# Moving one message and one distance step between the last filter products of a graph layer, and building the factors in one piece

## The chip, the cores and the metric

The kernel runs on one core of a Trainium2 chip. The metric is the device time of one execution in microseconds (us). The engines named here are TensorE (PE in the profile; its weight loads are PEld), VectorE (DVE), ScalarE (ACT), GpSimd (POOL) and SyncE (SP, which here only issues transfers). Each engine works through its own instructions in program order, and they wait for each other through semaphores.

## The reference, cut to what matters

There are 64 graphs of 256 nodes with 256 channels each. The layer normalizes, then computes a convolution branch, a message branch that is weighted by distances, and a GRU gate over both.

```python
h = jnp.maximum(_layernorm(x, axis=-1), 0.0)          # the layer's input, called x below
# convolution branch: 1x1, then 17 taps along the nodes
c = relu(bn1(conv1d(xc, conv1_w, 0)))
x_conv = relu(bn2(conv1d(c, conv2_w, 8)) + xc)
# message branch: 3 distance coordinates s of each node
s = x @ w_se.T + b_se
sq = jnp.sum(s * s, axis=-1)
dist = sq[:, :, None] + sq[:, None, :] - 2.0 * jnp.einsum('bnd,bmd->bnm', s, s)
A = jnp.exp(-dist) * mask                              # mask is adj
msg = relu(x @ w_msg.T + b_msg)
x_nmp = jnp.einsum('bnm,bmd->bnd', A, msg)
# gates
gi = concatenate([x_conv, x_nmp]) @ w_ih.T + b_ih
gh = x @ w_hh.T + b_hh
# ... r, z, n as in a GRU; out = x_input + (1 - z) * n + z * x
```

## The kernel before: the parts that are touched

The kernel takes graphs in pairs (G = 2), four pairs to a block, eight blocks. The 17 taps are evaluated by a fast transform over 16 positions: VectorE transforms a whole block, TensorE multiplies it by transformed filters (`products`, eight steps per block), and VectorE transforms back. The transformed filters are made once at the start by TensorE, in 57 small steps (`filter_steps`), and parked in DRAM (`filt`); each block reads them back (`wb`, nine buffers).

One filter step, with five `acc` buffers in PSUM and six `fo` buffers:

```python
def filters(m, g, eng):
    p = acc()
    for dc in range(DC):
        mm(p[...], points[m][...], taps[:size * TAPS, g, dc, :], D, start=True, stop=True)
    t = stage.tile([P, W], FP, name="fo", bufs=6)
    nc.scalar.copy(t[:size * kinds], p[:size * kinds])
    eng.dma_start(out=filt[m][...], in_=t[:size * kinds])   # gpsimd and sync in turn
```

The message of a pair, its distance factors, their transposition and the distances. `Z` holds the factors with nodes on partitions, `ZT` with factors on partitions; a block of 32 columns of `Z` belongs to one of the four chunks of 128 nodes of the pair:

```python
Z = const.tile([P, 2, G * MC, Q], FP, name="z")             # MC = 2 chunks, Q = 32
ZT = const.tile([P, (1 + MC) * P], FP, name="zT")

def message(i):
    for g in range(G):
        for c in range(MC):
            p = acc() if g * MC + c == 3 else aux()
            for k in range(DC):
                mm(p[:, :D + SE], chunk(HT[i][:, k], g, c), w_msg[:, k, :], ...)
            pace.vector(D, pace.pe + PSUM)
            nc.vector.tensor_add(MSG[i][:, g, c, :], p[:, :D + SE], b_msg)
    s = MSG[i][:, :, :, D:]
    flat = s.rearrange("p g c s -> p (g c) s")
    nc.scalar.mul(Z[:, 0, :, :SE], flat, -2.0)
    nc.scalar.activation(Z[:, 0, :, SE:2 * SE], flat, AF.Square)
    nc.scalar.copy(Z[:, 1, :, :SE], flat)
    nc.scalar.activation(Z[:, 1, :, 2 * SE:KD], flat, AF.Square)
    for g in range(G):
        nc.scalar.activation(MSG[i][:, g, :, :D], MSG[i][:, g, :, :D], AF.Relu)

def embed(i):
    p = aux()
    for j in range(2):
        transpose(p[:, j * P:(j + 1) * P], Z[:, j].rearrange("p q s -> p (q s)"))
    nc.scalar.copy(ZT[:, :P], p[:, :P])
    for q in range(G * MC):
        for c in range(MC):
            m = q // MC * MC + c
            nc.scalar.copy(ZT[q * Q:(q + 1) * Q, (1 + c) * P:(2 + c) * P], p[m * Q:(m + 1) * Q, P:2 * P])

def affinity(i):
    for g in range(G):
        for c in range(MC):                                  # q = g * MC + c
            nc.tensor.matmul(p[:, :N], ZT[rows_q, :P], ZT[rows_q, P:], start=True, stop=True)
            nc.scalar.activation(E[i][:, g, c], p[:, :N], AF.Exp, scale=-1.0)
    # ... VectorE multiplies the four results by adj
    if i + 1 < BY_DMA:
        load_adj(i + 1)                                      # issued by gpsimd into the one adj buffer
```

VectorE's order is set while the program is built. `pace` keeps an estimated clock of TensorE and of VectorE, and `pace.vector` puts queued transform steps ahead of an operation as long as they fit before the operation's input is ready.

The end of the start-up, and the first part of a block:

```python
forward()                                       # queues the first block's transform for VectorE
filter_steps(len(steps) - (NG - FIRST) - 4)     # 17 of the 57 steps are left after this
for n in range(3):
    for kind in range(3):
        load_kind(0, n, kind)                   # nine wb reads of 256 KB, by sync
filter_steps(len(steps))
# ...
pace.flush(odd)
for b in range(NB):
    i = b * PB
    message(i)
    pace.flush(odd)
    products(b, 0)
    embed(i)
    products(b, 1)
    pace.add(fft.branch_back(Yv, T, 0))
    affinity(i)
    if b > 0:
        load_adj(i + 1)
    products(b, 2)
    # ... further products, three more pairs' messages, the gates of four pairs
```

The third pair of each block has its `embed` and `affinity` inside the first gate, just before the convolution result `Yv` of the block's first pair is joined, scaled (DVE L788) and passed through a relu (ACT L789) for the gate product.

Of the kernel before, what the change touches and what calls it, by code (L numbers as in the profile page):

```python
# [13 lines left out]
FP = mybir.dt.float32  # L14
U16 = mybir.dt.uint16
AF = mybir.ActivationFunctionType
# [285 lines left out]
def kernel(  # L302
# [26 lines left out]
    nc = tc.nc  # L329
    P = 128  # L330
    B, N, D = x.shape
    G = 2
# [4 lines left out]
    MC = N // P  # L337
    W = G * N
    TAPS = c2_wT.shape[1]
    SE = se_wT.shape[1]  # L340
    KD = 3 * SE
    Q = 32
# [6 lines left out]
    const = ctx.enter_context(tc.tile_pool(name="const", bufs=1))  # L349
# [255 lines left out]
    s1, h1_shift = fold_bn(bn1, "bn1")  # L605


    Z = const.tile([P, 2, G * MC, Q], FP, name="z")
    nc.gpsimd.memset(Z, 0.0)
    nc.gpsimd.memset(Z[:, 0, :, 2 * SE:KD], 1.0)  # L610
    nc.gpsimd.memset(Z[:, 1:, :, SE:2 * SE], 1.0)
    ZT = const.tile([P, (1 + MC) * P], FP, name="zT")
# [110 lines left out]
    def load_kind(b, n, kind):  # L723
        b, n = b + n // BINS, n % BINS
        if b < NB and (n < BINS - 1 or kind < 2):
            WB[b, n, kind] = work.tile([P, DC, D], FP, name="wb", bufs=9)
            m = n // len(PASSES[0])
            nc.sync.dma_start(out=WB[b, n, kind], in_=filt[m][:, 3 * (n - PASSES[m][0]) + kind])
# [63 lines left out]
    def message(i):  # L792
        MSG[i] = work.tile([P, G, MC, D + SE], FP, name="msg")
# [4 lines that stand above are left out]
                    mm(p[:, :D + SE], chunk(HT[i][:, k], g, c), w_msg[:, k, :], D + SE,  # L798
                       start=(k == 0), stop=(k == DC - 1))
# [3 lines that stand above are left out]
        flat = s.rearrange("p g c s -> p (g c) s")  # L803
        nc.scalar.mul(Z[:, 0, :, :SE], flat, -2.0)
        nc.scalar.activation(Z[:, 0, :, SE:2 * SE], flat, AF.Square)
        nc.scalar.copy(Z[:, 1, :, :SE], flat)
        nc.scalar.activation(Z[:, 1, :, 2 * SE:KD], flat, AF.Square)
        for g in range(G):
            nc.scalar.activation(MSG[i][:, g, :, :D], MSG[i][:, g, :, :D], AF.Relu)

    def embed(i):
        p = aux()
        for j in range(2):
            transpose(p[:, j * P:(j + 1) * P], Z[:, j].rearrange("p q s -> p (q s)"))
        nc.scalar.copy(ZT[:, :P], p[:, :P])
        for q in range(G * MC):
            for c in range(MC):
                m = q // MC * MC + c  # L820
                nc.scalar.copy(ZT[q * Q:(q + 1) * Q, (1 + c) * P:(2 + c) * P], p[m * Q:(m + 1) * Q, P:2 * P])  # L821


    def affinity(i):
        E[i] = work.tile([P, G, MC, N], FP, name="e")
        for g in range(G):
            for c in range(MC):
                q = g * MC + c
                p = acc() if q == 3 else aux()
                rows_q = slice(q * Q, q * Q + KD)  # L830
                nc.tensor.matmul(p[:, :N], ZT[rows_q, :P], ZT[rows_q, P:], start=True, stop=True)  # L831
                nc.scalar.activation(E[i][:, g, c], p[:, :N], AF.Exp, scale=-1.0)
        pace.tensor(N)
        for g in range(G):
            for c in range(MC):
                pace.vector(N, pace.pe + ACT)
                e = E[i][:, g, c].rearrange("p (c h b) -> p c h b", c=MC, b=NW)
                nc.vector.tensor_mul(e, e, ADJ[i][:, g * MC + c].rearrange("p (b h c) -> p c h b", c=MC, b=NW))
        AT[i] = E[i]
        if i + 1 < BY_DMA:  # L840
            load_adj(i + 1)
# [113 lines left out]
    def filter_steps(n):  # L955
        for k in range(n):
            filters(*steps.popleft(), nc.gpsimd if len(steps) % 2 else nc.sync)
# [29 lines left out]
    for n in range(3):  # L987
        for kind in range(3):
            load_kind(0, n, kind)
    filter_steps(len(steps))  # L990
    stage_ctx.close()
    late = ctx.enter_context(tc.tile_pool(name="late", bufs=1, reuse_waits="tile"))
# [3 lines left out]
    for b in range(NB):  # L996
        i = b * PB
        nxt = i + PB
        message(i)
        pace.flush(odd)  # L1000
        products(b, 0)
        embed(i)
        products(b, 1)
        pace.add(fft.branch_back(Yv, T, 0))
        affinity(i)
        if b > 0:
            load_adj(i + 1)
        products(b, 2)
        if b > 0:
            finish(i - 1)  # L1010
        else:
            transpose_a(i)
        products(b, 3)
        pace.flush(even)
        if b == 0:
            norm(nxt)
        else:
            run(norm_steps(nxt + 1)[0])
        pace.add(fft.branch_back(Yv, T, 2))
        pace.add(fft.odd_back(Yv, T))  # L1020
        aggregate(i)
        if b > 0:
            join_adj(i + 1)
        else:
            nc.gpsimd.dma_start(out=w_hh, in_=hh_wT.rearrange("(k p) o -> p k o", p=P))
            nc.gpsimd.dma_start(out=w_ih, in_=ih_wT.rearrange("(k p) o -> p k o", p=P))
        products(b, 4)
        message(i + 1)
        products(b, 5, lambda i=i: embed(i + 1))
        pace.add(mix(fft.q_back(Yu, T), fft.odd_factors(Yv)))  # L1030
        if b == 0:
            pace.add(norm_steps(nxt + 1)[0], normed[1])
        affinity(i + 1)
        if b > 0:
            load_adj(i + 2)
            join_h(nxt)
        products(b, 6)
        if b == 0:
            transpose_a(i + 1)
            transpose_h(nxt)  # L1040
        products(b, 7)
        pace.add(mix(fft.p_back(Yu, T), fft.q_factors(Yu)), scaled)

        def join(j):
            pace.add(fft.join(Yu, Yv, T, slice(2 * G * j, 2 * G * (j + 1))))
            pace.add([(W, lambda o=o: residual(i + j, o)) for o in range(DC)], joined[j])
        join(0)
        pace.add(norm_steps(nxt + 2)[0], normed[2])
        join(1)
        if b == 0:  # L1050
            turn_adj(3)
            keep_adj(3)
        aggregate(i + 1)
        if b > 0:
            join_adj(i + 2)
        message(i + 2)
        pace.flush(normed[1])
        turn_h(nxt + 1)

        def wait():  # L1060
            pace.flush(scaled)
            affinity(i + 2)
            conv1(nxt, aux)
            pace.add(split_steps(nxt), halved)
            join(2)
            pace.flush(joined[0])
        gates(i, 0, wait, lambda i=i: embed(i + 2))
        if b == 0:
            transpose_a(i + 2)
            load_y(0)  # L1070
        load_adj(i + 3)
        sort_h(nxt + 1)
        turn_adj(nxt)
        keep_adj(nxt)

        def early():
            join_h(nxt + 1)
            pace.flush(normed[2])
            turn_h(nxt + 2)
        gates(i, 1, None, early)  # L1080
        pace.flush(halved)
        conv1(nxt + 1)
        join(3)
        pace.add(split_steps(nxt + 1), halved)
        pace.add(norm_steps(nxt + 3)[0], normed[3])
        aggregate(i + 2)
        join_adj(i + 3)
        pace.flush(joined[1])
        sort_h(nxt + 2)
        turn_adj(nxt + 1)  # L1090
        keep_adj(nxt + 1)
        gates(i + 1, 0, lambda nxt=nxt: join_h(nxt + 2))
        pace.flush(normed[3])
        turn_h(nxt + 3)
        pace.flush(halved)
        conv1(nxt + 2)
        pace.add(split_steps(nxt + 2), halved)
        pace.add(norm_steps(nxt + 4)[0], normed[0])
        finish(i)
        sort_h(nxt + 3)  # L1100
        turn_adj(nxt + 2)
        keep_adj(nxt + 2)
        gates(i + 1, 1)
        join_h(nxt + 3)
        message(i + 3)
        conv1(nxt + 3)
        pace.add(split_steps(nxt + 3), halved)
        if b + 1 < NB:
            forward()
        pace.flush(normed[0])  # L1110
        pace.flush(joined[2])

        def wait():
            affinity(i + 3)
            turn_h(nxt + 4)
        gates(i + 2, 0, wait, lambda i=i: embed(i + 3))
        sort_h(nxt + 4)
        turn_adj(nxt + 3)
        keep_adj(nxt + 3)
        aggregate(i + 3)  # L1120
        finish(i + 1)
        load_adj(nxt)
        gates(i + 2, 1)
        join_adj(nxt)
        pace.flush(joined[3])
        gates(i + 3, 0)
        finish(i + 2)
        gates(i + 3, 1)
# [45 lines left out]
```

## Time and profile before

| | before |
|---|---|
| time, median of 3 runs | 1835.29 us (1831.43 to 1835.35) |
| span of the profiled execution | 1833.5 us |
| TensorE matmul busy | 1793.6 us (98%) |
| VectorE busy | 1366.9 us (75%) |
| ScalarE busy | 765.7 us (42%) |
| GpSimd busy | 219.2 us (12%) |
| first product of the first block starts at | 107.06 us |
| length of each of the blocks two to seven | 215.87 us |

The profile has a page of sums for the whole span (busy time per engine, the span in slices, the chain of work that ended last, the costliest groups of instructions) and views that can be asked for a stretch: a timeline of one engine's instructions, the waits (who waited for whom), and windows (busy time by stretch, with the clock granted to TensorE as a share of full speed and the share of time the DMA engines were busy). In a timeline line, the first number is the start, the second the length from the first start to the last end, then engine, source line, operation, destination and source, shapes and count; brackets hold idle time before it and what ended that. Source line L517 is the helper through which nearly all matmuls go, so tiles tell them apart. Each fp32 matmul of the program appears as more than one record.

### The profile page before, as it was taken

How to read it: one execution, taken by the hardware profiler on the slowest of the kernel's cores; microseconds unless marked ns; L12 is line 12 of the kernel's file. 1: busy time of each engine (PE TensorE's matmuls, PEld its weight loads, DVE VectorE, ACT ScalarE, POOL GpSimd, SP SyncE). 2: the span in 40 equal slices, each digit the busy share in tenths (PEclk: the TensorE clock that was granted, in tenths of full speed). 3: DMA queues.
4: the chain of work that ended last, by engine and by line, in shares of the span. 5: the costliest groups of instructions: out<-in, count | busy, mean ns of one | idle time of the engine just before them, and what ended most of it. 6: DMA issues, size and time to landing. Idle time of an engine off the chain costs nothing.

```text
span 1833.5 us, 21931 instructions
## 1 busy us (share of the span) xinstructions
PE 1793.6 (98%) x7462; PEld 1108.4 (60%) x7462; DVE 1366.9 (75%) x2596; ACT 765.7 (42%) x1508; POOL 219.2 (12%) x357
## 2 busy tenths in 40 slices
PE   5999999999999999999999999999999999999998
PEld 3687454964559454784448645595546944487453
DVE  4879669795879849797697967888587984979422
ACT  2535541364323643255422653246432464225321
POOL 2210101100111011111012000110111110111000
PEclk9999999999999999999999999999999999999999
DMA  7778543854438444574347544384554744164011
GB/s 196 235 245 233 125 97 88 240 149 111 106 93 265 105 103 93 148 198 121 81 97 216 165 95 110 84 264 120 114 96 122 225 105 96 41 186 114 7 40 34
DMA packets 250483, 245.96 MB, mean 134 GB/s; under 512 B 142936, under 2 KB 176500, under 8 KB 250371
## 3 DMA queue, kind: packets, MB, share of 16 engines
q1 hardware_dynamic: 216634, 183.83, 36.5%
q0 software_dynamic: 30784, 58.07, 13.8%
q10 hardware_dynamic: 2953, 2.66, 0.7%
q8 instruction: 59, 0.97, 0.2%
q14 instruction: 53, 0.43, 0.1%
HBM read 156.56 MB, written 44.30 MB: 110 GB/s over the span
## 4 chain that ended last, share of the span: by engine, by line
PE 85%; ACT 5%; DVE 4%; issue 3%; DMA 1%; POOL 1%; ACTq 0%; POOLq 0%; DVEq 0%
PE acc L517 73%; PE aux L517 9%; PE aux L521 2%; ACT Yv L68 1%; ACT zT L821 1%; ACT adj L426 1%; PE aux L831 1%; ACT hh L648 1%; ACT V L68 1%; DVE Yv L65 1%; DMA taps<-in_c_wT_dram 1%; POOL filt L717 0%; DVE V L65 0%; DMA filt<-fo 0%; DVE T L62 0%
## 5 line engine op out<-in xcount | busy, mean ns | idle before, releaser
L517 PE MATMUL acc<-xnm,w_ih 128*128 128x512 f32 x768 | 353.1, 592 | 0.0
L517 PE MATMUL acc<-hT,w_hh 128*128 128x512 f32 x768 | 350.5, 592 | 0.0
L517 PE MATMUL acc<-Yv,w_ih 128*128 128x512 f32 x768 | 343.4, 597 | 6.7 <-ACT Yv L789 6.7
L517 PEld LDWEIGHTS acc<-Yv,w_ih 128*128 128x128 f32 x768 | 145.2, 191 | 192.7 <-issue 177.3
L517 PEld LDWEIGHTS acc<-xnm,w_ih 128*128 128x128 f32 x768 | 144.7, 190 | 176.0 <-issue 174.6
L517 PEld LDWEIGHTS acc<-hT,w_hh 128*128 128x128 f32 x768 | 143.9, 190 | 164.6 <-issue 155.5
L891 ACT ACTIVATE tr<-acc,b_rz 128x512 f32<-128x512 f32 x64 | 44.0, 687 | 346.6 <-PE acc L517 345.7
L893 DVE SCALAR_TENSOR_TENSOR gn<-tr,gn 128x512 f32<-128x512 f32 x64 | 44.2, 691 | 192.5 <-ACT tr L891 192.3
L927 POOL DMA_DIRECT2D out_dram<-y x62 | 38.2, 620 | 787.4 <-DVE y L926 762.3
L517 PE MATMUL acc<-V,wb 128*128 128x128 f32 x1024 | 124.8, 275 | 0.0
L517 PE MATMUL acc<-U,wb 128*128 128x128 f32 x1024 | 124.2, 276 | 0.0
L517 PEld LDWEIGHTS acc<-U,wb 128*128 128x128 f32 x1024 | 120.0, 192 | 3.6 <-DVE T L59 2.0
L59 DVE SCALAR_TENSOR_TENSOR V<-T,V 128x256 f32<-128x256 f32 (+2 forms) x224 | 121.7, 612 | 0.3
L517 PEld LDWEIGHTS acc<-V,wb 128*128 128x128 f32 x1024 | 119.5, 192 | 0.0
L517 PE MATMUL acc<-hT,w_c 128*128 128x512 f32 x228 | 107.4, 612 | 1.9 <-ACT hT L633 1.9
L517 PE MATMUL aux<-e,msg 128*128 128x256 f32 x464 | 104.9, 379 | 0.0
L517 PEld LDWEIGHTS aux<-e,msg 128*128 128x128 f32 x464 | 87.1, 190 | 17.7 <-issue 6.9
L898 ACT ACTIVATE nn<-gn,bn_columns 128x512 f32<-128x512 f32 x64 | 46.2, 722 | 115.5 <-DVE gn L896 115.5
L565 POOL TENSOR_TENSOR rstd<-rstd,neg_half 128x4 f32<-128x4 f32 x32 | 37.6, 1176 | 472.2 <-DVE shift L567 343.8
L517 PE MATMUL aux<-w_msg,hT 128*128 128x259 f32 x384 | 89.5, 382 | 0.0
L517 PEld LDWEIGHTS aux<-w_msg,hT 128*128 128x128 f32 x384 | 72.1, 190 | 17.5 <-issue 7.6
L426 ACT COPY adj<-adjh 128x1024 uint16<-128x1024 uint16 x58 | 74.0, 1346 | 19.3 <-DMA adjh<-halves_d 19.3
(164 smaller groups left out, 2725.8 us busy)
## 6 DMA issues: line engine op xcount, KB each, us to landing
wb<-filt SPq DMA_DIRECT2D x376, 256.0 KB
y<-in_x_dram POOLq DMA_DIRECT2D x64, 256.0 KB, 5.4
out_dram<-y POOLq DMA_DIRECT2D x62, 256.0 KB, 5.7
x<-in_x_dram SPq DMA_DIRECT2D x60, 256.0 KB
halves_d<-halves SPq DMA_DIRECT2D x116, 128.0 KB
adjh<-halves_d POOLq DMA_DIRECT2D x116, 128.0 KB, 5.6
hh<-halves SPq DMA_DIRECT2D x108, 128.0 KB
filt<-fo POOLq DMA_DIRECT2D x18, 252.0 KB, 5.3
```

What stands on the lines that cost most here:

```text
L59: return self.step(out, lambda: self.v.scalar_tensor_tensor(out, x, s, y, op0=ALU.mult, op1=ALU.add))
L65: return self.step(out, lambda: self.v.tensor_sub(out, x, y))
L68: return 0, lambda: self.a.mul(x, x, s)
L426: nc.scalar.copy(v[:, j], u[:, j])
L517: nc.tensor.matmul(p, w, v, **kw)
L521: nc.tensor.transpose(p, v, ident)
L565: nc.gpsimd.tensor_tensor(t["rstd"], t["rstd"], neg_half, ALU.pow)
L648: nc.scalar.activation(h[:, :, q], X[i][:, q, :].rearrange("p (k d) -> p k d", d=HP), AF.Relu, scale=STATS[i]["rstd"][:, q:q + 1], bias=ST ...
L891: nc.scalar.activation(tr, pr, AF.Tanh, bias=b_rz[:, dc:dc + 1], scale=0.5)
L893: nc.vector.scalar_tensor_tensor(gn, tr, 1.0, gn, op0=ALU.add, op1=ALU.mult)
L898: nc.scalar.activation(nn, gn, AF.Tanh, bias=b_ih[:, 2 * DC + dc:2 * DC + dc + 1])
L927: eng.dma_start(out=rows(out, G * i + g), in_=row_tile(Y[i], g))
```

## The change

Two things are changed. First, `Z` gets a third part, so that the right-hand factors are written in the place where each chunk needs them. `message` writes these by eight small ScalarE operations in place of two. `embed` then transposes three parts in place of two, and one ScalarE copy of 128 x 384 moves all of it, in place of nine copies (one 128 x 128 and eight of 32 x 128 that moved factors to other partitions). Second, the first pair's `message`, `embed` and `affinity` are taken out of the first block and put between the last 17 filter steps, to give TensorE other work there. With `affinity(0)` its issue of `load_adj(1)` moves as well.

```diff
-    Z = const.tile([P, 2, G * MC, Q], FP, name="z")
+    Z = const.tile([P, 1 + MC, G * MC, Q], FP, name="z")
@@ message
-        nc.scalar.copy(Z[:, 1, :, :SE], flat)
-        nc.scalar.activation(Z[:, 1, :, 2 * SE:KD], flat, AF.Square)
+        for c in range(MC):
+            z = Z[:, 1 + c].rearrange("p (g x) s -> p g x s", x=MC)
+            for x in range(MC):
+                nc.scalar.copy(z[:, :, x, :SE], s[:, :, c])
+                nc.scalar.activation(z[:, :, x, 2 * SE:KD], s[:, :, c], AF.Square)
@@ embed
-        for j in range(2):
+        for j in range(1 + MC):
             transpose(p[:, j * P:(j + 1) * P], Z[:, j].rearrange("p q s -> p (q s)"))
-        nc.scalar.copy(ZT[:, :P], p[:, :P])
-        for q in range(G * MC):
-            for c in range(MC):
-                m = q // MC * MC + c
-                nc.scalar.copy(ZT[q * Q:(q + 1) * Q, (1 + c) * P:(2 + c) * P], p[m * Q:(m + 1) * Q, P:2 * P])
+        nc.scalar.copy(ZT, p[:, :(1 + MC) * P])
@@ after the nine load_kind
+    message(0)
+    filter_steps(7)
+    embed(0)
+    filter_steps(4)
+    affinity(0)
     filter_steps(len(steps))
@@ in the loop over blocks
-        message(i)
+        if b > 0:
+            message(i)
         pace.flush(odd)
         products(b, 0)
-        embed(i)
+        if b > 0:
+            embed(i)
         products(b, 1)
         pace.add(fft.branch_back(Yv, T, 0))
-        affinity(i)
         if b > 0:
+            affinity(i)
             load_adj(i + 1)
```

## The prediction, made before the changed kernel was run

> **What bounds the kernel now.** I read the page first, then the waits of TensorE, then two stretches: the end of the start-up and the first gate of a block. The page has TensorE at 98% of the span. The start loses most of the rest, which windows of one block each show (columns: stretch, length, busy time of PE, PEld, DVE, ACT, POOL with counts, granted clock, DMA share, GB/s):
>
> ```profile
> 0.00:107.06 107.06, 82.84 (x311) 54.70 (x311) 66.21 (x143) 40.29 (x71) 27.83 (x54) 0.95 0.78 222
> 754.67:970.54 215.87, 215.30 (x897) 132.35 (x896) 169.07 (x320) 94.44 (x185) 25.53 (x40) 1.00 0.53 136
> ```
>
> A steady block has 215.87 - 215.30 = 0.57 us of TensorE idle, so there time goes down only by taking work off TensorE or by closing that gap. The waits of TensorE name what is left:
>
> ```profile
> PE acc L517 <- ACT Yv L789: 6.7, 8, 2.6
> PE acc L517 <- ACT fo L716: 3.8, 3, 2.5
> ```
>
> The second line is the end of the start-up. The timeline of TensorE there, then windows of 2 us:
>
> ```profile
> 89.70 2.81 PE L517 MATMUL acc<-taps,points 119*77 119x256 f32 x12 [0.21 <-ACT fo L716]
> 93.55 1.09 PE L517 MATMUL acc<-taps,points 119*77 119x256 f32 x4 [1.04 <-ACT fo L716]
> 97.17 6.34 PE L517 MATMUL acc<-taps,points 119*77 119x256 f32 x20 [2.54 <-ACT fo L716]
> 103.44 2.90 PE L517 MATMUL aux<-w_msg,hT 128*128 128x259 f32 x12
> ```
>
> ```profile
> 92.00:94.00 2.00, 0.96 (x5) 0.43 (x4) 2.00 (x4) 0.58 (x1) 0.14 (x1) 1.00 1.05 367
> 94.00:96.00 2.00, 0.64 (x3) 0.15 (x1) 2.00 (x5) 0.00 (x0) 0.00 (x0) 1.00 1.00 353
> 98.00:100.00 2.00, 2.00 (x6) 1.19 (x5) 0.00 (x0) 0.81 (x2) 0.53 (x1) 0.50 0.73 262
> ```
>
> The reader is to see three things. The filter steps wait for ScalarE, and ScalarE (0.58 us busy in two, then none) itself waits for a free `fo` buffer, while the DMA engines are full with the nine `wb` reads and the filter writes. TensorE loses 3.8 us in gaps. And after the gaps its clock is 0.50: the five filter steps from 97.17 take 6.3 us, against 5 x 0.87 = 4.4 us at full clock, another 1.9 us. VectorE, too, is idle from 98, waiting for the message.
>
> The first wait line is 0.57 us in six blocks, 0.67 in the first and 2.56 in the last. In the chain of waits of a steady block it is reached like this:
>
> ```profile
> 822.55 0.57 ACT gn L880
> 823.12 0.15 ACT zT L817
> 823.27 0.14 ACT zT L821
> ...
> 825.05 0.26 ACT zT L821
> 825.31 0.03 issue
> 825.33 0.63 ACT Yv L68
> 825.96 1.57 ACT V L68 x3
> ...
> 831.06 0.73 ACT Yv L789
> 831.79 0.04 issue
> 831.83 1.55 PE acc L517 x3
> ```
>
> The nine factor copies (zT) stand on this chain, from 823.12 to 825.31: 2.19 us of ScalarE time, followed by scaling, VectorE's joins and the relu that TensorE waits for.
>
> **What the Trainium skill says.** "TensorE: Matmul & The Clock Gate", section "What's actually happening": the array falls to half clock after an idle window of about 3.4 us and needs about as long of work to recover. The trace agrees in kind: clock 0.50 after a stretch with 3.6 us of gaps between 92.5 and 97.2. "Perfetto Trace Analysis", section "Optimizing Scalar/DVE Operations": each operation carries a fixed access cost, so grouping into larger ones helps a saturated engine. The trace agrees: a 32 x 128 copy costs 0.26 us, while two 128 x 512 copies from PSUM take 1.07 us with a single one at 0.58, a step of 0.49 for four times the columns. The same page, "Optimization Strategy", recommends interleaving regimes with different bounds; here a stretch held by transfers gets work that needs none.
>
> **The change part by part.**
>
> Step 1, steady, TensorE: one more transposition per pair. Two take 0.22 us on the chain, so one is 0.11 us; 31 pairs outside the start-up give **+3.4 us**. Nothing hides it, as TensorE is the bound.
>
> Step 2, steady, ScalarE: the nine copies (2.19 us) become one of 128 x 384. Between the steps of 0.28 us (128 x 256, the exponentials) and 0.49 us (128 x 512) it should cost about 0.39 us: -1.8 us. The factor operations in `message` grow from 4 to 10; the chain shows 0.09 to 0.12 us each: +0.6 us. Net -1.2 us per pair. It counts only on the chain of the first gate, which exceeds the 0.57 and 0.67 us waits; both should vanish: 6 x 0.57 + 0.67 = 4.1 us. In the last block ScalarE waits for the transposition itself, so the longer `message` is hidden there and the copy brings 1.8 of the 2.56 us. Sum **-5.9 us**. VectorE doesn't hold the chain: it idles 2.9 to 3.6 us before its joins.
>
> Step 3, the start: filter step 41, before which `message(0)` now stands, begins on TensorE at about 82.0 us (the 36th `fo` copy, which frees its accumulator, ends at about 81.9). From there the work is 17 filter steps of 0.87 us (14.8), the message (3.6, from 103.44 to 107.06), three transpositions (0.33) and four distance products (0.64 on the chain): 19.4 us. Without any gap the first products begin at 101.4. I count 0.6 us of leftover stalls: the ScalarE copies stand behind the message's relus until about 88, run again into `fo` buffers held by writes at about 94, but five accumulators (4.3 us of filter steps) bridge most of it. So 102.0. Before, they began at 107.06 and had 0.22 + 0.64 us of transposition and distances still to come among them: 107.06 + 0.86 - 102.0 = 5.9 us. Because this balance of queues is the least certain part I take **-5.3 us**.
>
> Step 4, VectorE in the start: four additions of 0.34 us and four multiplications by adj (2.1 us) enter its queue earlier. By the pace estimate the additions land near 82 us, two or three small steps before the odd transform ends. Its idle 8.1 us before the first message addition (104.62) disappears, so the transform's even part finishes earlier, not later: 0 us on the path.
>
> Sum: +3.4 - 5.9 - 5.3 = -7.8 us, 1835.3 - 7.8 = **1827.5 us**.
>
> **The rivals.**
>
> Transfers keep the end of the filters. If 2.3 MB of `wb` reads and about 3 MB of filter writes, and not TensorE's idling, set the last filter step, it still ends at 103.4, and only the moved work is hidden: 3.6 + 0.86 = 4.5 us from the start, total near 1828. For it: DMA share 1.0 from 88 to 96. Against it: from 100 to 102 the share is 0.35 while TensorE works at low clock.
>
> A new queue jam. ScalarE works in order, so the message's factor operations wait for VectorE with filter copies behind them; and GpSimd's `load_adj(1)` waits for the multiplications with filter writes behind it. The latter holds only the last three GpSimd writes, whose buffers no later step needs. If TensorE idles 3 us again and its clock falls, the start gains only 1 to 2 us: total near 1831.
>
> Another releaser follows in the gate. If the join on VectorE or the first convolution's eviction ends the wait as late as before, step 1 stands alone in the steady part (+3.4): total near 1833. The idle time of VectorE before the joins speaks against it.
>
> The other way, a start without leftover stalls and the last block's wait gone altogether would give about 1826.
>
> **Range and chances.** The steps are worth a few microseconds each and partly opposed; a 2% change would need 36.7 us, more than the whole TensorE idle time after the first 15 us. The three runs before spread over 3.9 us, half of my effect. I take 1823.5 to 1832 as the range that should hold it 8 times in 10. Faster by over 2%: 0.005; within 2%: 0.99; slower by over 2%: 0.005.
>
> **What would show it right or wrong.** Step 1: groups of transpositions of z at x96 instead of x64, three in 0.33 us, and steady blocks with 0.43 us more TensorE work. Step 2: the wait for Yv L789 near zero in blocks one to seven and 0.8 us in the last; a steady block of 215.7 us. Step 3: first product at 101.5 to 103, gaps before `fo` under 1 us, clock 1.00 in windows from 92 to 102. Step 4: VectorE with no idle of 8 us before the message. The prediction is wrong if the first product starts later than 105, if a steady block is longer than 215.87, or if a new wait (for `wb`, or for VectorE's even transform before the fifth product step) appears in the first block.

## The result, and the profile after

| | before | after |
|---|---|---|
| time, median of 6 runs each | 1835.62 us (1831.43 to 1837.11) | 1829.83 us (1828.26 to 1831.30) |
| ratio | | 0.9971, 95% interval 0.9958 to 0.9984 |
| span of the profiled execution | 1833.5 us | 1829.2 us |
| first product of the first block | 107.06 us | 105.78 us |
| filter step 41 (after: the message ahead of it) to the first product | 25.0 us | 24.7 us |
| a steady block | 215.87 us | 215.63 us |

The time fell by 0.29%, about 5.3 us by the ratio (2.9 to 7.7), where 7.8 us had been forecast. The two profiles differ by 4.3 us: 1.3 before the first product, 1.6 in the first block, which no longer holds the first pair's transposition and distances (0.86 us on the chain before), and 0.24 in each of the six blocks that follow. First the steady part: the windows of one block of the kernel after, in the columns shown for before.

```profile
828.31:1043.94 215.63, 215.59 (x901) 132.79 (x900) 169.10 (x322) 89.63 (x177) 25.35 (x40) 1.00 0.52 136
```

The 0.57 us gap is gone (215.63 - 215.59 = 0.04), and TensorE's busy time rose by 0.3 us: a gap was exchanged for work on the bounding engine. The waits of TensorE after:

```profile
PE acc L517 <- ACT Yv L789: 1.9, 1, 1.9
PE aux L829 <- ACT zT L819: 1.7, 1, 1.7
PE acc L517 <- ACT fo L716: 1.3, 1, 1.3
```

Of eight waits for Yv one is left, in the last block. The other two are in the start: the factor copy is new, the filter copy was there before. There, the timeline of TensorE shows how far the interleaving carried:

```profile
81.11 2.80 PE L517 MATMUL aux<-w_msg,hT 128*128 128x259 f32 x12
...
91.27 3.62 PE L517 MATMUL acc<-taps,points 119*77 119x256 f32 x16
96.63 0.49 PE L829 MATMUL aux<-zT 9*128 9x256 f32 x3 [1.75 <-ACT zT L819]
...
98.65 7.20 PE L517 MATMUL acc<-taps,points 119*77 119x256 f32 x24 [1.31 <-ACT fo L716]
105.78 1.16 PE L517 MATMUL acc<-Sv,wb 128*128 128x128 f32 x8
```

TensorE works without a gap until 94.9, then loses 1.75 and 1.31 us, and the last six filter steps take 7.20 us. ScalarE's timeline says what it waited for:

```profile
90.46 0.58 ACT L716 COPY fo<-acc 77x512 f32<-77x512 f32 x1 [0.42 <-DMA filt<-fo]
95.62 0.58 ACT L716 COPY fo<-acc 77x512 f32<-77x512 f32 x1 [4.58 <-DMA filt<-fo]
96.10 0.48 ACT L819 COPY zT<-aux 128x384 f32<-128x384 f32 x1
98.02 2.03 ACT L716 COPY fo<-acc 77x512 f32<-77x512 f32 x4 [1.44 <-DMA filt<-fo]
```

The factor copy (zT) at 96.10 is short, but it stands in ScalarE's order behind filter copy 47, which waits 4.58 us for a `fo` buffer. It is the stall of before, at nearly the same time. Copy 47 takes the buffer of step 42, whose write GpSimd issues:

```profile
88.67 0.53 POOL L717 DMA_DIRECT2D filt<-fo  x1 [4.10 <-ACT fo L716]
```

This write landed at 95.5, 6.9 us after its issue (the median of GpSimd's writes of this size is 5.0), while the DMA share was 0.96 to 1.02 (windows from 90 to 96). The chain of waits after names the transfers behind the next copy, 48 (start, length, what):

```profile
82.64 0.38 SPq L728
83.02 0.06 issue
83.08 8.19 DMA wb<-filt
91.27 0.02 issue
91.28 0.02 SPq L717
91.30 0.46 issue
91.76 6.18 DMA filt<-fo
97.94 0.02 issue
97.96 0.02 ACTq L716
97.98 0.04 issue
98.02 0.59 ACT fo L716
98.61 0.04 issue
98.65 23.47 PE acc L517 x168
```

SyncE issues the nine reads and every second filter write, in order. The write of step 41 was issued only at 91.76, when all nine reads were out and the second of them had landed (91.27), and it landed at 97.9; copy 48 takes its buffer. So one write was held in SyncE's order; the other went out at once and was slow to land while the DMA engines were full. And the clock, in windows of 2 us, fell again:

```profile
94.00:96.00 2.00, 0.89 (x5) 0.30 (x3) 2.00 (x4) 0.38 (x1) 0.00 (x0) 1.00 0.96 369
100.00:102.00 2.00, 2.00 (x6) 1.15 (x5) 1.64 (x4) 1.90 (x7) 0.38 (x1) 0.50 0.85 248
```

### The profile page after: what moved, and what is told of

The parts are those of the page before. It is cut to its first block, busy times and chain, and to the rows that moved or that the text cites. A ratio compares the mean times of both kernels' runs of the same rounds, so it can differ in the third digit from the quotient of the medians.

```text
span 1829.2 us, 21881 instructions
## 1 busy us (share of the span) xinstructions
PE 1794.1 (98%) x7494; PEld 1112.1 (61%) x7494; DVE 1367.0 (75%) x2596; ACT 727.6 (40%) x1444; POOL 220.7 (12%) x357
## 4 chain that ended last, share of the span: by engine, by line
PE 93%; DMA 3%; DVE 2%; ACT 1%; issue 0%; SPq 0%; ACTq 0%; DVEq 0%
PE acc L517 80%; PE aux L517 10%; PE aux L521 2%; DMA taps<-in_c_wT_dram 2%; PE aux L829 1%; DMA filt<-fo 1%; DVE Yv L59 1%; DMA wb<-filt 0%; DVE T L65 0%; DVE Yv L62 0%; DVE msg L801 0%; ACT fo L716 0%; DVE st L559 0%; DVE Yv L771 0%; DVE V L772 0%
```

## The experiments

Ratios are to the kernel before, run on the same chip. The theory after the result: the steady part did about what was worked out, and the start gained little because six `fo` buffers fill while the reads hold the filter writes. Rivals: ScalarE's order (the message's operations ahead of filter copies), the transfers' total bandwidth, or a wrong place for the message.

**Each half of the change alone.** The first kernel keeps the new factors and puts the first pair back behind the filter steps; the second keeps the move and restores the old factors.

```diff
 # z_only
-    message(0)
-    filter_steps(7)
-    embed(0)
-    filter_steps(4)
-    affinity(0)
     filter_steps(len(steps))
 # ... and message, embed, affinity in the block without "if b > 0"
 # move_only: Z with 2 parts, 4 factor operations, 2 transpositions, 9 copies
```

> The changed kernel with the first pair left in its old place: only the third part of Z, the ten small factor operations, three transpositions and one copy. Theory A (the steady part brings about half of the gain: one block went from 215.87 to 215.64 us, the last wait from 2.56 to 1.88): about 2 us below the kernel before, near 1833.5, first product unchanged near 107. Theory B (nearly the whole gain is in the start, the steady part only breaks even): within 0.7 us of the kernel before. Theory C (the start gave nothing and the steady part all of it): 5 to 6 us below, near 1830.

> The kernel before with only the first pair's message, factors and distances between the filter steps; two transpositions and nine copies as before. Theory A: 2 to 4 us below the kernel before, first product near 105.8, with the same wait for a filter write of 4 to 5 us on ScalarE as in the changed kernel, steady blocks of 215.87 us. Theory B: 5 to 6 us below. Theory C: no gain.

Measured: new factors alone 1832.29 us, ratio 0.9988 (0.9981 to 0.9996), or 2.2 us less; the move alone 1831.01 us, ratio 0.9980 (0.9972 to 0.9988), or 3.7 us less. The two add up to the change (0.32% against 0.29%). Theory A holds for the totals. Two of its details do not: with the new factors alone the first product came at 108.53 us, not near 107, after 6.8 us at half clock in place of 3.4, and with the move alone at 104.37, not 105.8. With the move alone all eight waits for Yv are there (6.7 us), and the start still has gaps, smaller ones than in the changed kernel's profile: 0.27, 0.40 and 0.90 us, from step 41 (here the message begins at 80.07) to the first product 24.3 us. ScalarE's longest wait for a filter write was 2.9 us, not the expected 4 to 5.

**Twelve buffers.** The six additional ones lie in the space of the gate weights, which are loaded later.

```diff
 # fo12
-        t = stage.tile([P, W], FP, name="fo", bufs=6)
+        k = len(SENT) % 12
+        SENT.append(k)
+        if k < 6:
+            t = stage.tile([P, W], FP, name="fo", bufs=6)
+        else:
+            t = w_ih.rearrange("p k d -> p (k d)")[:, (k - 6) * W:(k - 5) * W]
```

> The changed kernel with twelve buffers for the filter steps' results in place of six (the six more lie in the gate weights' space, which is filled later). Theory T (the start gained little because six buffers fill up while the nine reads of 2.4 MB hold the filter writes: copies 47 and 48 waited for writes 41 and 42): ScalarE's waits for filter writes near zero, TensorE without gaps and at full clock from 81 to 101, first product at 101 to 102, total 4 to 5 us below the changed kernel, near 1825. Rival R (ScalarE's order is the cause: the factor operations and relus of the message stand ahead of the filter copies): the same gaps, no gain. Rival S (the transfers' bandwidth sets the end whatever the buffers): the gaps move to a wait for wb reads or to the first products, total within 1.5 us of the changed kernel.

Measured: 1824.83 us, ratio 0.9945 (0.9930 to 0.9960), 5.0 us below the changed kernel by the medians. The timeline of TensorE of this kernel:

```profile
78.29 2.79 PE L517 MATMUL aux<-w_msg,hT 128*128 128x259 f32 x12
...
92.64 5.51 PE L517 MATMUL acc<-taps,points 119*77 119x256 f32 x24
98.08 1.16 PE L517 MATMUL acc<-Sv,wb 128*128 128x128 f32 x8
```

From the message to the first product it takes 98.08 - 78.29 = 19.8 us, where 19.4 had been counted for a start without gaps; six filter steps take 5.51 us in place of 7.20, at full clock. ScalarE's order is unchanged here, so rival R falls as a cause by itself; the reads and writes are the same bytes, so rival S falls too. The first product is earlier than the expected 101 to 102 because the message had begun early: at 78.29, against 80.48 and 80.54 in two kernels below that are the same up to there. All three take 19.8 us from there on.

**The reads spread out**, one after every second filter step, with six buffers:

```diff
 # reads_spread
+            if reads and len(steps) % 2 == 0:
+                load_kind(0, *reads.popleft())          # inside filter_steps
```

> The changed kernel with six buffers, but the nine wb reads are issued one after every second of the last 17 filter steps in place of all before the first of them. Theory T (the block of nine reads holds the writes): waits of ScalarE for filter writes fall from about 7 us to 1 to 3, first product at 102 to 103, total 3 to 4 us below the changed kernel. Rival R: no gain. Rival S: filter steps end earlier, but the first products wait for their reads, total within 1.5 us of the changed kernel.

Measured: 1830.39 us, ratio 0.9970 (0.9960 to 0.9980): nothing over the changed kernel, where theory T had 3 to 4 us. Message to first product took 20.9 us (80.84 to 101.71), so the block of reads did hold the writes, though not alone: ScalarE still waited 6.9 us for filter writes between 76 and 108 us (10.0 in the changed kernel), not 1 to 3. And what the start gained the first block lost (220.68 us against 216.97), since the products wait for their reads, as these lines of the waits of TensorE and of the windows show:

```profile
PE acc L517 <- DMA wb<-filt: 2.1, 2, 1.3
```

```profile
86.00:88.00 2.00, 2.00 (x10) 0.98 (x8) 2.00 (x2) 2.00 (x6) 0.00 (x0) 1.00 0.00 0
```

From 86 to 88 us the DMA engines move nothing (share 0.00): the spread reads stand in SyncE's order behind filter writes whose copies ScalarE does only after the message's relus. The early block of reads used that time. The total and the waits for reads came as rival S said, but the idle DMA engines show that the order of issue has a part, and not bandwidth alone; it pays to let reads run early and give the writes room.

**The old place, with twelve buffers.**

```diff
 # fo12_old_place = z_only with fo12's buffers: message(0), embed(0), affinity(0) back in the block
```

> Twelve buffers and the new factors, but the first pair's message, factors and distances back in their old place behind the last filter step. Theory T (the filter steps lose time only to full buffers; moving work among them is worth something only while there are gaps to fill): no gaps of TensorE before the message, the same work in another order, total within 1 us of the kernel with twelve buffers and the moved work, near 1825. Rival M (the interleaving is worth something by itself, because it lets VectorE and ScalarE start early or because the reads are further ahead): 2 to 4 us slower than it, near 1828.

Measured: 1824.08 us, ratio 0.9938 (0.9923 to 0.9954), no slower than with the move (1824.83). Its timeline has one unbroken row of filter steps, then the message:

```profile
73.78 22.13 PE L517 MATMUL acc<-taps,points 119*126 119x256 f32 x100
95.84 2.90 PE L517 MATMUL aux<-w_msg,hT 128*128 128x259 f32 x12
```

The intervals (about 0.15% each way) are too wide to exclude rival M's 2 us by themselves. The profiles settle it: from the start of step 41, or of the message ahead of it, to the first product of the second block, the kernel takes 236.78 us with the old place and 236.75 with the move. On the same measure the kernel before takes 243.54 and the changed kernel 241.64. So the move is worth something only while there are gaps to fill.

**The message later among the filter steps**, six buffers:

```diff
 # msg_later
-    message(0)
-    filter_steps(7)
+    filter_steps(9)
+    message(0)
+    filter_steps(4)
     embed(0)
-    filter_steps(4)
+    filter_steps(2)
     affinity(0)
```

> The changed kernel with six buffers, with the message after 9, the factors after 13 and the distances after 15 of the last 17 filter steps, so that TensorE reaches the message about when ScalarE has run out of buffers. Theory T (buffers and held writes set the pace, not the place of the work): from filter step 41 to the first product about 23.5 us, at most 1.5 us less than the 24.7 us of the changed kernel; total within 1.5 us of it. Rival P (the message simply stood in the wrong place): about 20.5 us, total 3 to 4 us below the changed kernel.

Measured: 1828.94 us, ratio 0.9966 (0.9950 to 0.9982), within 1 us of the changed kernel. The waits for buffers came back in smaller pieces: ScalarE waited nine times for filter writes, 12.1 us in all, and the first product began at 104.87. Counted back through the records, step 41 begins at 80.7, so 24.2 us: theory T, not P. To the first product of the second block it took 241.78 us (241.64 in the changed kernel).

**One more transposition alone**, on the kernel before:

```diff
 # third_t, in embed
+        transpose(p[:, 2 * P:3 * P], Z[:, 1].rearrange("p q s -> p (q s)"))
```

> The kernel before with one more transposition per pair, whose result nothing reads; all copies as before. Step 1 alone: 0.11 us on TensorE in each of 32 places, less where it only shortens a wait (the one before the gate): steady block 216.1 to 216.3 us, total 2.5 to 3.5 us above the kernel before. Rival (a transposition is hidden by weight loads or waits): no difference.

Measured: 1838.14 us, ratio 1.0016 (1.0009 to 1.0024), or 2.9 us more. A steady block has 216.11 us, 0.24 more, where four transpositions make 0.44: one of them shortened the wait for Yv (0.57 to 0.46), and the second pair's distance products, 0.73 us in the kernel before, took 0.64. From the first product to the end the profile is only 2.0 us longer; the rest of its difference lies in the start, where this run had 13.7 us at half clock against 3.4.

**One copy alone**, on the kernel before; it leaves out the eight copies between partitions:

```diff
 # one_copy, in embed; ZT is set to zero once at the start
-        nc.scalar.copy(ZT[:, :P], p[:, :P])
-        for q in range(G * MC): ...                     # the eight copies
+        nc.scalar.copy(ZT[:, :2 * P], p[:, :2 * P])
```

> The kernel before with two transpositions and one copy of 128 x 256 in place of the nine; the third part of ZT stays zero, so the distances are not the reference's. It leaves out the eight copies between partitions and nothing else. Step 2 alone: the wait for Yv vanishes in blocks one to seven (steady block 215.1 to 215.3 us) and falls to about 1.9 us in the last, total 5 to 6 us below the kernel before. Rival (the join, the eviction or the exponentials end the wait as late): steady block above 215.6.

Measured: 1827.92 us, ratio 0.9956 (0.9941 to 0.9971). Its steady block, in the window columns:

```profile
614.92:829.88 214.96, 214.96 (x898) 132.34 (x897) 168.91 (x321) 87.12 (x152) 25.24 (x40) 1.00 0.54 136
```

The block lost 0.91 us, not 0.57. Here the wait cost more than the idle time shown for it: from the start of the last group before it to the start of the first after it the timeline has 2.45 us with the wait and 1.72 without, that first group itself took 5.42 us in place of 5.31, and the second pair's distance products took 0.64 us in place of 0.73 here too. With 0.44 us for four transpositions the changed kernel's block should then be 214.96 + 0.44 = 215.40 us; it is 215.63. The missing 0.23 us is in one place, the second pair's transposition (timeline of TensorE of the changed kernel):

```profile
786.32 2.80 PE L517 MATMUL aux<-w_msg,hT 128*128 128x259 f32 x12
788.95 1.04 PE L517 MATMUL acc<-w_msg,hT 128*128 128x259 f32 x4
789.83 2.84 PE L517 MATMUL acc<-U,wb 128*128 128x128 f32 x24
792.50 0.76 PE L521 MATMUL aux<-ident,z 128*128 128x128 f32 x3
```

Everywhere else in the block three transpositions take 0.49 us. Here, 2.7 us after the message, they take 0.76; the weight loads of TensorE wait seven times in the whole run for the last of the ten factor operations, 1.8 us in all.

**The last block's wait.** In the changed kernel's chain it reads:

```profile
1687.30 0.21 PE aux L829 x3
1687.50 0.04 PE acc L829
1687.55 0.13 ACT e L830
1687.68 0.13 issue
1687.81 0.93 ACT e L830 x3
1688.74 0.61 ACT Yv L789
1689.35 0.04 issue
1689.39 0.70 PE acc L517
```

The factor copies have left the chain. The relu (L789) now stands behind the four exponentials in ScalarE's order, and these wait for TensorE's own distance products. The next kernel, on fo12, turns that order round in the last block; the one after it, on top, writes the eight small factor operations as four.

```diff
 # fo12_exp_later, in wait()
             pace.flush(scaled)
-            affinity(i + 2)
+            if b + 1 < NB:
+                affinity(i + 2)
             conv1(nxt, aux)
             pace.add(split_steps(nxt), halved)
             join(2)
             pace.flush(joined[0])
+            if b + 1 == NB:
+                affinity(i + 2)
 # six_ops, in message
-            for x in range(MC):
-                nc.scalar.copy(z[:, :, x, :SE], s[:, :, c])
-                nc.scalar.activation(z[:, :, x, 2 * SE:KD], s[:, :, c], AF.Square)
+            sc = s[:, :, c].unsqueeze(2).broadcast_to([P, G, MC, SE])
+            nc.scalar.copy(z[:, :, :, :SE], sc)
+            nc.scalar.activation(z[:, :, :, 2 * SE:KD], sc, AF.Square)
```

> Twelve buffers and the moved work, and in the last block alone the distances of the third pair are placed behind the join of the first, so that the relu for the gate product stands ahead of the four exponentials in ScalarE's order. Theory E (in the changed kernel's last block the relu waits for the exponentials, and these for TensorE's own distance products, so that the shortened copy could not bring its 1.8 us): the wait of TensorE for Yv there falls from 1.9 to about 0.6 us, total 1 to 1.5 us lower. Rival (VectorE's join sets it): the wait stays at 1.9.

> The kernel with twelve buffers, moved work and later exponentials, with the eight small factor operations written as four (each reads a chunk's three coordinates twice). Theory Z (in the changed kernel the factor operations grew from 4 to 10, and at the second pair's transposition, which follows its message by only 2.7 us, TensorE waits about 0.27 us per block for the last of them): the transposition group there shrinks from 0.76 to 0.49 us, a steady block goes from 215.6 to about 215.4 us, total 1 to 2 us lower than with ten operations, 1821 to 1822. Rival (the 0.27 us is due to VectorE's message additions): the group stays at 0.76.

Measured: the first 1822.80 us, ratio 0.9927 (0.9914 to 0.9940), 2.0 us less than fo12 by the medians, where 1 to 1.5 had been expected (the intervals of the two overlap), with this left of the wait (TensorE's waits):

```profile
PE acc L517 <- ACT Yv L795: 0.6, 1, 0.6
```

The second 1819.67 us, ratio 0.9904 (0.9890 to 0.9918): the steady block went to 215.4 us and the second pair's transpositions to their usual length (timeline line below), as theory Z has it. The time is 3.1 us less than the first by the medians, more than the 1 to 2 expected; the blocks show 0.25 us each, and the rest was not traced. It is the best kernel of the study, 0.96% below the kernel before.

```profile
787.42 0.49 PE L521 MATMUL aux<-ident,z 128*128 128x128 f32 x3
```

## Why the prediction was right, and where its terms were off

The time lies within 1823.5 to 1832, and the signs of the first three steps held; the sum was 2.5 us too large, and the larger error was in the step that was called least certain.

Step 1, +3.4 us: 2.9 us measured alone (1.7 to 4.4). The term is right where no wait hides it: four transpositions add 0.44 us of work to a block. Alone they made a block only 0.24 us longer, so part of the agreement of the totals is luck.

Step 2, -5.9 us: alone, the shortened copy brought 8.1 us (5.3 to 10.8, from 0.9956; 6.5 by the medians), an interval that includes the forecast. Two errors inside it were opposite. In the steady blocks the gap was taken as 0.57 us and was worth 0.91. In the last block 1.8 us were expected and 0.7 came (2.56 to 1.88), because another releaser followed. That rival had been named in general, with the wrong candidates: it was neither VectorE's join nor the convolution's eviction, but the exponentials ahead of the relu. And the cost of four to ten factor operations was only weighed on the chain of the first gate, where the copy's saving covered it; at the second pair's transposition it is a wait of its own, some 0.25 us per block. Steps 1 and 2 together, -2.5 us, were measured at -2.2 (0.7 to 3.5). That this is so near is luck: the block came to 215.63 us, where the prediction had 215.7, because the larger worth of the gap (0.34 us more) and the wait that had been overlooked nearly cancelled.

Step 3, -5.3 us: -3.7 with the move alone (2.2 to 5.1), about -3.1 as the difference between the change and the new factors alone (0.9971 and 0.9988). In the profiles, which both have one stretch of 3.4 us at half clock there, the move alone shortened the way from step 41 to the second block by 1.7 us (243.54 to 241.85); where the rest of the 3.7 lies is not shown. TensorE did work through part of the old gaps, but the term "0.6 us of leftover stalls" was too small: from the message to the first product it took 24.7 us, 5.3 over the 19.4 counted. Of that 3.1 us are the two gaps, 1.7 us the half clock after them (7.20 - 5.51), and 0.4 us the count itself, since the kernel without gaps took 19.8. The prediction had the filter copies come against held writes and five accumulators (4.3 us) bridge most of it. But the writes of steps 42 and 41 landed 7 and 10 us after their copies, and ScalarE held the factor copy for the distances behind them as well. By its own signs (a first product later than 105, gaps before `fo` of 1 us or more, a clock under 1.00 before 102 us) this step failed in size.

The rival "a new queue jam" came nearest: it had TensorE idle 3 us again, its clock fall, the start gain 1 to 2 us and a total near 1831. TensorE idled 3.1 us, the clock was 0.50, and the first product came 1.3 us earlier and the total was 1829.8. But the cause it names, ScalarE's order and the message in it, does not make the jam by itself: the kernel before has the jam without it, and twelve buffers remove the jam with it. Whether that order deepens the jam with six buffers was not tested alone. The rival "transfers keep the end of the filters" falls with the twelve buffers, where the same bytes let the filters end 19.8 us after the message's start.

Step 4, 0 us: VectorE's message additions began at 82.19, three small transform steps and a last large one before the end of the odd part, nearly as worked out, and the 8.1 us of idling went. The even part nevertheless ended later (119.3 against 117.0), because 4.2 us of waiting for the exponentials took its place; with the fifth product step at 131.7 that cost nothing.

## What to carry to other kernels

When an engine idles behind full buffers, ask first what more buffers would do: filling the gap with moved work and removing the gap are two uses of the same time, and here the second, with six more buffers, brought the larger part and made the first worth nothing. When a chain is shortened, look for the next instruction in the same engine's order, not only for the next in the data flow; the factor copy of 0.48 us stood behind a filter copy that waited 4.58. And count small operations where their result is needed soonest, not only on the chain that is longest now.

## What the runs showed of the hardware that was not expected

No single gap of TensorE among the last 17 filter steps exceeded 2.6 us, yet stretches at half clock of very different length followed in kernels with the message in its old place and six buffers: 3.4 us in the profile of the kernel before, 6.8 with the new factors alone, 13.7 with the third transposition, where even the message ran slowly:

```profile
105.72 5.55 PE L517 MATMUL aux<-w_msg,hT 128*128 128x259 f32 x12
```

That is 5.55 us against 2.90. The lengths are multiples of the window of about 3.4 us that the Trainium skill states in "TensorE: Matmul & The Clock Gate", "What's actually happening". In the four kernels with twelve buffers no such stretch followed the start's filter steps, and none in two with six: with the reads spread out (one gap, 0.58 us) and with the message later (gaps of up to 1.62 us). With the move alone, though, gaps of at most 0.90 us were followed by one of 3.4. Nor need the same gap have the same result: after the wait of 1.9 us in the last block a stretch of 3.4 us followed in the changed kernel and in the one with twelve buffers, and none with one copy alone or with twelve buffers and the old place. Where that wait was 0.6 us none followed, which may be why the kernel with the later exponentials gained more than expected.

Such stretches go with a good part of the spread: over 41 runs of the kernel before on one chip, time and mean clock have a correlation of -0.70, about half of the variance. The three with a mean clock of 0.993 had a median of 1837.2 us, sixteen with 0.995 one of 1834.6, and two with 0.997 one of 1832.9. One window more or less at half clock costs 1.7 us, so a comparison of single profiles (4.3 us here) can miss the mean gain (5.3) by that.
